# A graph layer with mixture-of-experts attention: the last tiles of z transposed in halves between gates and the first queries and keys

## The chip, the cores and the metric

The kernel runs on one core of a Trainium2 chip, in one launch. The metric is the device time of the execution in microseconds (us), the median of several runs. A core has five engines with instruction streams of their own: TensorE (PE in the profile; its weight loads are PEld), VectorE (DVE), ScalarE (ACT), GpSimd (POOL) and SyncE (SP), which here issues most of the DMAs. An engine executes its stream in order, so an instruction that waits holds up everything behind it on its engine.

## The reference

1250 nodes with 1024 values each go through a graph layer and then through an attention layer whose values and outputs are mixtures of experts:

```python
edge_index = stack([src, dst])                      # 40000 edges, and one self loop per node
x  = x + gnn(layernorm(x), edge_index, W, b)        # h = x W^T + b; sum over edges, weighted by degrees^-1/2
z  = layernorm(x)                                   # x is called x1 in the kernel
q  = rope(einsum('bsd,hdp->bhsp', z, Wq))           # 16 heads of 64
k  = rope(einsum('bsd,hdp->bhsp', z, Wk))
gv = gate(z, Wsel_v); go = gate(z, Wsel_o)          # sigmoid scores of 8 experts, all but the best two set to 0
v  = einsum('bsd,bhse,hedp->bhsp', z, gv, Wv)
o  = softmax(q k^T / 8) v
y  = z + einsum('bhsp,bhse,hepd->bsd', o, go, Wo)
y  = layernorm(y, ln1_g, ln1_b)
y  = layernorm(y + relu(y W1 + b1) W2 + b2, ln2_g, ln2_b)
out = x + y
```

## The kernel before

All large products are made in three matmuls: each operand is split into a rounded part (`hi`, type fp32r) and what is left (`lo`), and `dot` (L152 to L156) adds hi x hi, hi x lo and lo x hi in a PSUM tile. A split costs a copy on ACT (the rounding) and a subtraction on DVE (the rest): for a weight block of 128x1024, loaded by SP into a raw buffer of `w_raw` (two of them), they are L138 and L144; for a transposed tile they are L190 and L191.

**Stages in order of time.** The edges are counted into a matrix `at16`, beside h = W x + b (to 232 us). `sums(ts)` (L478) makes the graph sums of tile t of 125 nodes: 40 matmuls of 512 columns, then on DVE the scaling and the residual (`x1`, in a buffer named `y`), and the layer norm (`normalize`: two `bn_stats` and their aggregate, a square root on ACT, the reciprocal, the last step), which gives z. Both x1 and z are stored to DRAM (`x1_d`, `z_d`; each `move` is two DMAs, of 112 and of 13 rows). The last sum's matmul ends on PE at 314.05 us.

What follows needs z with its 1024 values on the partitions: `turn_z` (L520) calls `transposed` (L181), which takes a tile in two halves, each of four PE transposes (L187) into one bank of `side` (PSUM, three banks in turn), one ACT copy into `hi` and one DVE subtraction into `lo` (a tile that straddles columns 512 has two of each). The result is `zT`, in two pieces: zT00/zT01 for the first `CUT` = 512 nodes and zT10/zT11 for the other 738. The first four of ten tiles are turned during the sums (L527 to L531). The other six come after them: `rest_of_z` (L542) loads each from `z_d` into a `w_raw` buffer and turns it.

- `queries_keys` (L599) has 48 pieces: 16 blocks of weights (`wqk`, 8 pairs of heads, two halves of their dimensions), and for each three column chunks of 512, 384 and 354 nodes. A piece is 8 x 3 matmuls into one of four `mm` banks, then the rotation by cos and sin for every other block (L643 to L648, four DVE operations), the split and the regrouping (L649 to L658); after a third chunk the results go to DRAM (`kq_d`).
- `gates` (L551) has ten pieces: 8 x 3 matmuls of 256 columns for 128 nodes (`dot` L580, in a `side` bank), the sigmoid on ACT (L583), then 14 DVE operations that find the two best of eight (`pick`, L558, twice, and L585 to L590), the product for the values' gates (`gate_v`), and one for the outputs' gates, which `turn_gates` (L568) transposes one gate later into `po` and ACT copies into `gT`. Its weights `wsel` are two blocks, split at its start (L556).

**Order.** L678 to L683 set the order in which these are issued: first tile 4 of z, then the other five between the first two pieces of queries and keys, then a gate after every third piece. But in this stage the order written is no more than a priority: a scheduler with a cost model places the instructions of every engine. From the attention on (`attention`, `values`, `outputs`) the order of every engine is written by hand (`tc.manual_schedule`, L1106); the last part (`outputs`' rest from L1131 and `feed_forward`, L1031: layer norm, two products with 512 hidden values, layer norm and residual) is left to the scheduler again. There L1018 adds each finished output product to `acc` on DVE.

**Buffers.** Weight parts come from `ring`, a list of pools used in turn: two slots of `ring0` and, after the sums, three of `ring1` (L533). `hpool` holds h in two parts and two z tiles.

Of the kernel before, what the change touches and what calls it, by code (L numbers as in the profile page):

```python
# [72 lines left out]
def gnn_ffn_kernel(  # L73
# [106 lines left out]

    def transposed(targets, y, psum_tile):  # L181

        for half in range(2):
            p = psum_tile([P, 4, KT])
            for k in range(4):
                d0 = (4 * half + k) * P
                nc.tensor.transpose(p[:, k, :], y[:, d0 : d0 + P], ident[:KT, :KT])  # L187
            for hi, lo, c0, cols in targets:
                to = (slice(None), slice(4 * half, 4 * half + 4), slice(c0, c0 + cols.stop - cols.start))
                nc.scalar.copy(hi[to], p[:, :, cols])  # L190
                nc.vector.tensor_tensor(lo[to], p[:, :, cols], hi[to].bitcast(F32), ALU.subtract)  # L191

    def broadcast_row(pool, row, name):

        b = pool.tile([P, D], F32, name=name)
        nc.sync.dma_start(b, bass.AP(tensor=row.tensor, offset=row.offset, ap=[[0, P], [1, D]]))
        return b


    with ExitStack() as gctx:  # L200
# [277 lines left out]
        def sums(ts):  # L478
# [19 lines left out]
            for t, pp in zip(ts, pps):  # L498
                x1 = stream.tile([P, D], F32, name="y")
                move(x1, xres_d[t])  # L500
                for half in range(2):
                    cols = slice(512 * half, 512 * half + 512)
                    nc.vector.scalar_tensor_tensor(x1[:KT, cols], pp[half], ds[:KT, t : t + 1], x1[:KT, cols],
                                                   op0=ALU.mult, op1=ALU.add)
                z = hpool.tile([P, D], F32, name="z", bufs=2)
                normalize(z[:KT], x1[:KT], "g")
                move(z_d[t], z)
                move(x1_d[t], x1)
                zs.append(z)
# [9 lines left out]

        def turn_z(t, z):  # L520

            c0, c1 = KT * t, KT * (t + 1)
            mid = min(max(CUT, c0), c1)
            targets = [(*zT[k], a - CUT * k, slice(a - c0, b - c0)) for k, a, b in ((0, c0, mid), (1, mid, c1)) if b > a]
            transposed(targets, z, side_bank)

        for t in range(2, NT):  # L527
            new = sums([t])
            if t - 2 < NZ:
                turn_z(t - 2, zs.pop(0)[:KT])  # L530
                zs += new  # L531

    ring += [ctx.enter_context(tc.tile_pool(name="ring1", bufs=3))] * 3  # L533
    zpool2 = z2_ctx.enter_context(tc.tile_pool(name="zpool2", bufs=1, side="right"))
# [6 lines left out]

    def rest_of_z():  # L542

        for t in range(NZ, NT):
            z = raws[0].tile([P, D], F32, name="w_raw")[:KT]
            move(z, z_d[t])
            turn_z(t, z)
            yield


    def gates(wpool, tmp):  # L551
        first_wins = wpool.tile([P, NX], F32, name="first_wins")
        nc.gpsimd.iota(first_wins, pattern=[[-1, NX]], base=NX, channel_multiplier=0,
                       allow_small_or_imprecise_dtypes=True)
        gT = wpool.tile([P, N], F32, name="gT")
        sel = [weights(wsel[k]) for k in range(2)]  # L556

# [15 lines left out]

        before = None
        for t in range(NT):
            n = min(P, N - P * t)
            p = side_bank([n, 2 * P])
            for d in range(ND):
                w = [part[:, 2 * P * (d % 4) : 2 * P * (d % 4 + 1)] for part in sel[d // 4]]
                dot(p, z_of(t, d), w, d == 0, d == ND - 1)  # L580
            s, a, b, c = (tmp.tile([P, 2 * H, NX], F32, name=k)[:n] for k in ("s", "a", "b", "chosen"))
            m = tmp.tile([P, 2 * H], F32, name="m")[:n]
# [7 lines left out]
            nc.vector.tensor_tensor(a[:, H:, :], s[:, H:, :], c[:, H:, :], ALU.mult)  # L590
            if before is not None:
                turn_gates(t - 1, before)
            before = a
            yield
        turn_gates(NT - 1, before)
        nc.sync.dma_start(g_d, gT)


    def queries_keys(tab, work):  # L599
        cos_s = tab.tile([P, N], F32, name="cos_s")  # L600
        nc.sync.dma_start(cos_s, cos)
        sin_s = tab.tile([P, N], F32, name="sin_s")
        nc.sync.dma_start(sin_s, sin)
        turn16 = [(i + NROT // 2) % NROT for i in range(NROT)]
# [19 lines left out]
        pieces = [(i, k) for i in range(H) for k in range(3)]  # L624
        pieces[:6] = [(0, 0), (1, 0), (0, 1), (0, 2), (1, 1), (1, 2)]
        tiles = {}
        for i, k in pieces:
# [7 lines left out]
            for d in range(ND):  # L635
                dot(p, [part[:, P * d : P * (d + 1)] for part in w],
                    [part[:, d, c0 : c0 + n] for part in zT[part2]], d == 0, d == ND - 1)
            at_ = slice(CUT * part2 + c0, CUT * part2 + c0 + n)
            if other:
# [38 lines left out]
    with tc.tile_pool(name="qktab", bufs=1) as tab, tc.tile_pool(name="qkwork", bufs=2) as work, \  # L678
            tc.tile_pool(name="gatet", bufs=2) as tmp:
        turns, rest = queries_keys(tab, work), rest_of_z()  # L680
        next(rest)
        interleave(islice(turns, 2), rest, 1, 2 / 5)
        interleave(turns, gates(tab, tmp), 1, 3)  # L683

# [524 lines left out]
```

## Time and profile before

| | |
|---|---|
| median of 3 runs | 2961.8 us (2959.9 to 2963.07) |
| profiled execution, its own time | 2961.16 us |
| its span, first to last instruction | 2959.4 us |
| mean granted TensorE clock | 0.986 |
| PE busy | 2849.7 us (96%), 14018 instructions |
| DVE busy | 2120.9 us (72%), 3588 |
| ACT busy | 993.0 us (34%), 1706 |
| POOL busy | 569.1 us (19%), 945 |
| DMA | 385.45 MB, mean 130 GB/s |

By stages: sums to 314.05 us, the last tiles of z and first queries and keys to 364, queries, keys and gates to 591.6, values, attention and outputs to about 2780, the last part to 2959.

How the lines are read: a page's engine rows give 40 equal slices of the span (74 us each), each digit the busy share in tenths. A row of the time line is start, duration, engine, line of the code, operation, output tile <- inputs, shape, and in brackets the idle time of the engine before it and whose result ended it. A row of waits is the waiting engine, tile and line, the instruction it waited for, and the sum, number and longest of the waits. `PEclk` is the granted TensorE clock, 1.00 being full speed. Matmuls overlap in the pipeline, so a matmul's duration is longer than its distance from the one before; that distance is what counts when PE is full.

### The profile page before, as it was taken

The page shows a single profiled execution, that of the slowest core. Times are in us where ns is not written, and L with a number is a line of the kernel's source. Part 1 is how long each engine was busy: PE and PEld are TensorE (multiplying, and loading weights), DVE is VectorE, ACT ScalarE, POOL GpSimd, SP SyncE. Part 2 cuts the span into 40 slices and gives each one's busy share as a digit, 9 for nine tenths or more (in the row PEclk, how much of TensorE's full clock was granted, in tenths as well). Part 3 has the DMA queues.
Part 4 walks back from the last instruction along what each step waited for, and adds up shares of the span by engine and source line. Part 5 has one row for each costly group of instructions (what it writes and reads, how often), then busy time and mean ns, then how long its engine had stood idle before and what let it go on. Part 6 is the DMA issues. An engine that isn't in the chain of part 4 may idle for free. (4 is left out here: it accounts for less than half of the span.)

```text
span 2959.4 us, 40398 instructions
## 1 busy us (share of the span) xinstructions
PE 2849.7 (96%) x14018; PEld 2349.2 (79%) x14018; DVE 2120.9 (72%) x3588; ACT 993.0 (34%) x1706; POOL 569.1 (19%) x945
## 2 busy tenths in 40 slices
PE   6989899999999999999999999899999999999998
PEld 4767699978887887788888888777777777777787
DVE  7974487647777777778778787866666666656885
ACT  5772233324343433434434344321111111111222
POOL 2000011113333333333333333310000000000113
PEclk9999899999999999999999999999999999999999
DMA  3114456644555554555555555884444444444312
GB/s 117 56 44 146 150 163 169 197 99 125 151 132 134 134 142 124 144 140 147 130 152 139 144 132 129 209 217 128 114 119 121 114 123 117 115 121 119 112 52 88
DMA packets 229320, 385.45 MB, mean 130 GB/s; under 512 B 43369, under 2 KB 176489, under 8 KB 228946
## 3 DMA queue, kind: packets, MB, share of 16 engines
q1 hardware_dynamic: 176898, 273.49, 33.3%
q0 software_dynamic: 51888, 104.18, 14.6%
q10 hardware_dynamic: 320, 5.12, 0.6%
q8 instruction: 111, 1.82, 0.3%
q14 instruction: 103, 0.84, 0.1%
HBM read 220.73 MB, written 62.16 MB: 96 GB/s over the span
## 5 line engine op out<-in xcount | busy, mean ns | idle before, releaser
L154 PE MATMUL mm<-w_hi,go_hi 128*125 128x512 f32 x1280 | 507.9, 397 | 4.5 <-DVE zT L1018 3.4
L155 PE MATMUL mm<-w_lo,zT 128*128 128x512 f32 (+1 forms) x1280 | 506.4, 396 | 4.3 <-DVE w_lo L144 3.9
L155 PE MATMUL mm<-w_lo,go_hi 128*125 128x512 f32 x1280 | 508.8, 398 | 0.0
L154 PE MATMUL mm<-w_hi,zT 128*128 128x512 f32 (+1 forms) x1280 | 506.5, 396 | 1.0 <-ACT w_hi L138 1.0
L156 PE MATMUL mm<-w_hi,go_lo 128*125 128x512 f32 x1280 | 506.7, 397 | 0.7 <-DVE go_lo L960 0.7
L156 PE MATMUL mm<-w_hi,zT 128*128 128x512 f32 (+1 forms) x1280 | 505.3, 395 | 0.0
L755 ACT CAST att_hi<-turned 128x512 fp32r<-128x512 f32 x400 | 239.5, 621 | 455.5 <-DVE turned L798 279.5
L736 POOL DMA_DIRECT2D turned<-p x640 | 342.5, 542 | 80.8 <-ACT p L725 44.3
L1018 DVE TENSOR_TENSOR zT<-zT,mm 125x512 f32<-125x512 f32 x256 | 175.5, 686 | 220.5 <-PE mm L156 216.3
L798 DVE STREAM_TRANSPOSE turned<-turned 128x1280 f32<-128x1280 f32 x160 | 232.4, 1490 | 135.7 <-DMA q<-kq_d 57.5
L958 ACT CAST go_hi<-gb 128x500 fp32r<-128x500 f32 x160 | 98.3, 615 | 660.1 <-PE mm L155 289.1
L724 DVE TENSOR_REDUCE most<-side 128x1 f32<-128x1250 f32 x160 | 231.0, 1444 | 108.2 <-PE side L721 106.7
L725 ACT ACTIVATE p<-side,most 128x1250 f32<-128x1250 f32 x160 | 209.2, 1307 | 289.4 <-DVE most L724 284.7
L154 PEld LDWEIGHTS mm<-w_hi,go_hi 128*125 128x125 f32 x1280 | 239.1, 187 | 66.0 <-DVE zT L1018 4.1
L156 PEld LDWEIGHTS mm<-w_hi,go_lo 128*125 128x125 f32 x1280 | 238.9, 187 | 61.9 <-DVE go_lo L960 1.2
L155 PEld LDWEIGHTS mm<-w_lo,go_hi 128*125 128x125 f32 x1280 | 238.7, 186 | 59.2
L156 PEld LDWEIGHTS mm<-w_hi,zT 128*128 128x128 f32 (+1 forms) x1280 | 238.0, 186 | 59.5
L155 PEld LDWEIGHTS mm<-w_lo,zT 128*128 128x128 f32 (+1 forms) x1280 | 238.4, 186 | 44.3 <-DVE w_lo L144 9.4
L154 PEld LDWEIGHTS mm<-w_hi,zT 128*128 128x128 f32 (+1 forms) x1280 | 238.3, 186 | 35.8 <-ACT w_hi L138 1.2
L760 DVE TENSOR_TENSOR att_lo<-turned,att_hi 128x512 fp32r<-128x512 f32 x400 | 262.4, 682 | 0.0
L778 PE MATMUL po<-att_hi,v 128*128 128x256 f32 (+1 forms) x800 | 215.0, 290 | 33.8 <-ACT o L785 33.5
L144 DVE TENSOR_TENSOR w_lo<-w_raw,w_hi 128x1024 fp32r<-128x1024 f32 x154 | 189.5, 1231 | 43.6 <-ACT w_hi L138 43.3
(234 smaller groups left out, 4611.3 us busy)
## 6 DMA issues: line engine op xcount, KB each, us to landing
turned<-p SPq DMA_DIRECT2D x640, 80.0 KB
turned<-p POOLq DMA_DIRECT2D x640, 80.0 KB, 3.3
gb<-g_d SPq DMA_DIRECT2D x160, 250.0 KB
w_raw<-in_wv SPq DMA_DIRECT2D x64, 512.0 KB
w_raw<-in_wo SPq DMA_DIRECT2D x64, 512.0 KB
q<-kq_d POOLq DMA_DIRECT2D x80, 256.0 KB, 4.3
oc<-o_d SPq DMA_DIRECT2D x160, 125.0 KB
kq_d<-qk_hi SPq DMA_DIRECT2D x64, 156.2 KB
```

What stands on the lines that cost most here:

```text
L144: (lo_engine or nc.vector).tensor_tensor(lo, raw, hi.bitcast(F32), ALU.subtract)
L154: nc.tensor.matmul(p, lhsT=lhs[0], rhs=rhs[0], start=start, stop=False)
L155: nc.tensor.matmul(p, lhsT=lhs[0], rhs=rhs[1], start=False, stop=False)
L156: nc.tensor.matmul(p, lhsT=lhs[1], rhs=rhs[0], start=False, stop=stop)
L724: nc.vector.tensor_reduce(most, side[:, :N], AX.X, ALU.max, negate=True)
L725: nc.scalar.activation(p[:, (2 * n + i) % 3, :N], side[:, :N], AF.Exp, bias=most, accum_out=inverse[h][:, 2 * c + i : 2 * c + i + 1])
L736: queue.dma_start(t[NB * a : NB * (a + 1), :, KA * b : KA * (b + 1)], both[NB * b : NB * (b + 1), :, KA * a : KA * (a + 1)])
L755: nc.scalar.copy(hi, x)
L760: nc.vector.tensor_tensor(lo, x, hi.bitcast(F32), ALU.subtract)
L778: nc.tensor.matmul(po, lhsT=v_of[h][:rows, t, :], rhs=part[:rows, :, NB * b : NB * (b + 1)], start=(first and b == 0 and part is parts[0]) ...
L798: nc.vector.transpose(turned[n][:, i], turned[n][:, i])
L1018: nc.vector.tensor_tensor(acc[t][:, cols], acc[t][:, cols], p, ALU.add)
```

## The change

- `transposed` and `turn_z` take the halves that they are to do. `rest_of_z(pool)` goes on by half tiles, and loads each z tile two tiles ahead of its use, into two buffers `z` of the pool `tmp` (that of the gates' small tiles) instead of the `w_raw` buffers.
- The gates' weights `wsel` are loaded and split during the sums, when tile 5 of them is issued, into the two slots of `ring0`; for queries and keys the ring has only the three slots of `ring1`, and `ring0` is put back after. For room, z tiles 6 to 9 of the sums are made in `w_raw` buffers. `first_wins` (the order in which equal scores win) is made at the kernel's start.
- A gate takes an `mm` bank instead of a `side` bank, and is transposed three gates later, with four `a` buffers.
- A piece of queries and keys can be left after half of its matmuls; the first six pieces stand in another order. The tables cos and sin are loaded after the first gate.
- In the stretch after the sums PE's order is written by hand (`manual_schedule` for PE alone; the other engines stay with the scheduler): gates, half tiles and half pieces in turn, by the tuple `order`. After it, a gate comes after every sixth half piece.

As built, PE's order after the last sum is: gate 0, half tile 4a, gate 1, 4b, gate 2, 5a, half a piece, 5b, half, 6a, gate 3, 6b, half, 7a, half, 7b, 8a, half, 8b, half, 9a, half, 9b, half, and so on. Every half tile waits for the DVE subtraction of the half before it. z tile 4's load waits for the last graph sum on PE, tile 6's for tile 4's second half. SP issues in the order: z tile 4, tile 5, x1's last store, a `wqk` block, z's last store, cos, sin, z tile 6, two `wqk` blocks, tile 7, two more blocks, tiles 8 and 9. On ACT, gate 0's sigmoid stands ahead of the last normalisation's square root. The instructions of attention, values and outputs stand in the same order as before up to the last 40 output matmuls, ahead of which 23 of the feed-forward's first matmuls now come.

```diff
@@ -178,9 +178,9 @@
         nc.vector.scalar_tensor_tensor(out, x, mean, scale, op0=ALU.subtract, op1=ALU.mult)
         nc.vector.scalar_tensor_tensor(out, out, rs, shift, op0=ALU.mult, op1=ALU.add)
 
-    def transposed(targets, y, psum_tile):
-
-        for half in range(2):
+    def transposed(targets, y, psum_tile, halves=(0, 1)):
+
+        for half in halves:
             p = psum_tile([P, 4, KT])
             for k in range(4):
                 d0 = (4 * half + k) * P
@@ -195,6 +195,9 @@
         b = pool.tile([P, D], F32, name=name)
         nc.sync.dma_start(b, bass.AP(tensor=row.tensor, offset=row.offset, ap=[[0, P], [1, D]]))
         return b
+
+    first_wins = base.tile([P, NX], F32, name="first_wins")
+    nc.gpsimd.iota(first_wins, pattern=[[-1, NX]], base=NX, channel_multiplier=0, allow_small_or_imprecise_dtypes=True)
 
     with ExitStack() as gctx:
@@ -502,7 +505,7 @@
                     cols = slice(512 * half, 512 * half + 512)
                     nc.vector.scalar_tensor_tensor(x1[:KT, cols], pp[half], ds[:KT, t : t + 1], x1[:KT, cols],
                                                    op0=ALU.mult, op1=ALU.add)
-                z = hpool.tile([P, D], F32, name="z", bufs=2)
+                z = hpool.tile([P, D], F32, name="z", bufs=2) if t < 6 else raws[0].tile([P, D], F32, name="w_raw")
                 normalize(z[:KT], x1[:KT], "g")
                 move(z_d[t], z)
                 move(x1_d[t], x1)
@@ -517,20 +520,24 @@
         zpool = z_ctx.enter_context(tc.tile_pool(name="zpool", bufs=1, side="right"))
         zT = [[zpool.tile([P, ND, CUT], F32R, name=f"zT0{k}") for k in range(2)]]
 
-        def turn_z(t, z):
+        def turn_z(t, z, halves=(0, 1)):
 
             c0, c1 = KT * t, KT * (t + 1)
             mid = min(max(CUT, c0), c1)
             targets = [(*zT[k], a - CUT * k, slice(a - c0, b - c0)) for k, a, b in ((0, c0, mid), (1, mid, c1)) if b > a]
-            transposed(targets, z, side_bank)
+            transposed(targets, z, side_bank, halves)
 
         for t in range(2, NT):
             new = sums([t])
+            if t == 5:
+                sel = [weights(wsel[k]) for k in range(2)]
             if t - 2 < NZ:
                 turn_z(t - 2, zs.pop(0)[:KT])
                 zs += new
 
-    ring += [ctx.enter_context(tc.tile_pool(name="ring1", bufs=3))] * 3
+
+    first_two = ring[:]
+    ring[:] = [ctx.enter_context(tc.tile_pool(name="ring1", bufs=3))] * 3
     zpool2 = z2_ctx.enter_context(tc.tile_pool(name="zpool2", bufs=1, side="right"))
     zT.append([zpool2.tile([P, ND, N - CUT], F32R, name=f"zT1{k}") for k in range(2)])
 
@@ -539,21 +546,23 @@
         k = t if t < NZ else t - NZ
         return [part[:, d, P * k : min(P * (k + 1), part.shape[2])] for part in zT[t >= NZ]]
 
-    def rest_of_z():
-
-        for t in range(NZ, NT):
-            z = raws[0].tile([P, D], F32, name="w_raw")[:KT]
-            move(z, z_d[t])
-            turn_z(t, z)
-            yield
+    def rest_of_z(pool):
+
+        zs = []
+        for t in range(NZ - 2, NT):
+            if t >= NZ:
+                turn_z(t, zs[0], (0,))
+                yield
+                turn_z(t, zs.pop(0), (1,))
+            if t + 2 < NT:
+                zs.append(pool.tile([P, D], F32, name="z")[:KT])
+                move(zs[-1], z_d[t + 2])
+            if t >= NZ:
+                yield
 
     def gates(wpool, tmp):
-        first_wins = wpool.tile([P, NX], F32, name="first_wins")
-        nc.gpsimd.iota(first_wins, pattern=[[-1, NX]], base=NX, channel_multiplier=0,
-                       allow_small_or_imprecise_dtypes=True)
         gT = wpool.tile([P, N], F32, name="gT")
-        sel = [weights(wsel[k]) for k in range(2)]
 
         def pick(chosen, v, m):
 
@@ -571,14 +580,15 @@
             nc.tensor.transpose(pg, a[:, H:, :].rearrange("p h e -> p (h e)"), ident[:n, :n])
             nc.scalar.copy(gT[:, P * t : P * t + n], pg)
 
-        before = None
+        before = []
         for t in range(NT):
             n = min(P, N - P * t)
-            p = side_bank([n, 2 * P])
+            p = bank([n, 2 * P])
             for d in range(ND):
                 w = [part[:, 2 * P * (d % 4) : 2 * P * (d % 4 + 1)] for part in sel[d // 4]]
                 dot(p, z_of(t, d), w, d == 0, d == ND - 1)
-            s, a, b, c = (tmp.tile([P, 2 * H, NX], F32, name=k)[:n] for k in ("s", "a", "b", "chosen"))
+            s, a, b, c = (tmp.tile([P, 2 * H, NX], F32, name=k, bufs=4 if k == "a" else 2)[:n]
+                          for k in ("s", "a", "b", "chosen"))
             m = tmp.tile([P, 2 * H], F32, name="m")[:n]
             nc.scalar.activation(s.rearrange("p h e -> p (h e)"), p, AF.Sigmoid)
             pick(c, s, m)
@@ -588,19 +598,16 @@
             nc.vector.tensor_tensor(gate_v[:n, t, :].rearrange("p (h e) -> p h e", h=H), s[:, :H, :], c[:, :H, :],
                                     ALU.mult)
             nc.vector.tensor_tensor(a[:, H:, :], s[:, H:, :], c[:, H:, :], ALU.mult)
-            if before is not None:
-                turn_gates(t - 1, before)
-            before = a
+            before.append(a)
+            if t > 2:
+                turn_gates(t - 3, before.pop(0))
             yield
-        turn_gates(NT - 1, before)
+        for t in range(NT - 3, NT):
+            turn_gates(t, before.pop(0))
         nc.sync.dma_start(g_d, gT)
 
-    def queries_keys(tab, work):
-        cos_s = tab.tile([P, N], F32, name="cos_s")
-        nc.sync.dma_start(cos_s, cos)
-        sin_s = tab.tile([P, N], F32, name="sin_s")
-        nc.sync.dma_start(sin_s, sin)
+    def queries_keys(cos_s, sin_s, work):
         turn16 = [(i + NROT // 2) % NROT for i in range(NROT)]
 
         chunks = [(0, 0, CUT), (1, 0, 3 * P), (1, 3 * P, N - CUT - 3 * P)]
@@ -622,7 +629,7 @@
 
         pieces = [(i, k) for i in range(H) for k in range(3)]
-        pieces[:6] = [(0, 0), (1, 0), (0, 1), (0, 2), (1, 1), (1, 2)]
+        pieces[:6] = [(0, 0), (1, 0), (0, 1), (1, 1), (0, 2), (1, 2)]
         tiles = {}
         for i, k in pieces:
             j, other = divmod(i, 2)
@@ -635,6 +642,8 @@
             for d in range(ND):
                 dot(p, [part[:, P * d : P * (d + 1)] for part in w],
                     [part[:, d, c0 : c0 + n] for part in zT[part2]], d == 0, d == ND - 1)
+                if d == ND // 2 - 1:
+                    yield
             at_ = slice(CUT * part2 + c0, CUT * part2 + c0 + n)
             if other:
                 raw, scale = p, HD**-0.5
@@ -677,10 +686,19 @@
 
     with tc.tile_pool(name="qktab", bufs=1) as tab, tc.tile_pool(name="qkwork", bufs=2) as work, \
             tc.tile_pool(name="gatet", bufs=2) as tmp:
-        turns, rest = queries_keys(tab, work), rest_of_z()
-        next(rest)
-        interleave(islice(turns, 2), rest, 1, 2 / 5)
-        interleave(turns, gates(tab, tmp), 1, 3)
+        cos_s, sin_s = (tab.tile([P, N], F32, name=name) for name in ("cos_s", "sin_s"))
+        turns, rest, gate = queries_keys(cos_s, sin_s, work), rest_of_z(tmp), gates(tab, tmp)
+
+        order = (gate, rest, gate, rest, gate, rest, turns, rest, turns, rest, gate, rest, turns, rest, turns, rest,
+                 rest, turns, rest, turns, rest, turns, rest, turns)
+        with tc.manual_schedule(engines={mybir.EngineType.PE}):
+            next(gate)
+            nc.sync.dma_start(cos_s, cos)
+            nc.sync.dma_start(sin_s, sin)
+            for what in order[1:]:
+                next(what)
+        interleave(turns, gate, 1, 6)
+    ring[:0] = first_two
```

## The prediction

> **What bounds the kernel now.** I read the page first, for which engine is full and where not, then the table by stretches around the change, then who TensorE waited for there, then the time line of that stretch.
>
> ```profile
> PE 2849.7 (96%) x14018; PEld 2349.2 (79%) x14018; DVE 2120.9 (72%) x3588; ACT 993.0 (34%) x1706; POOL 569.1 (19%) x945
> ...
> PE   6989899999999999999999999899999999999998
> ```
>
> TensorE (PE) sets the time: 96% busy, and its slices are full except at the start and in the fifth slice (296 to 370 us, an 8). Two stretches of the table by stretches, the columns being named in its header:
>
> ```profile
> core 0: us, PE busy (x) PEld busy (x) DVE busy (x) ACT busy (x) POOL busy (x), PEclk, DMA share, GB/s
> 314.05:364.00 49.95, 35.99 (x152) 29.48 (x151) 22.34 (x39) 13.87 (x24) 0.14 (x1) 0.79 0.36 120
> 364.00:591.60 227.60, 226.93 (x1301) 212.14 (x1300) 174.27 (x388) 75.38 (x158) 29.29 (x60) 1.00 0.61 176
> ```
>
> 314.05 is where the last graph sum ends on PE, 591.6 where the first value product begins. In the first stretch, which I call the head, PE is idle for 14.0 of 49.95 us and its granted clock is 0.79; VectorE (DVE) is 45% busy, and the DMA engines move 120 GB/s. After it PE is full. PE's waits in the head:
>
> ```profile
> PE side L187 <- DVE zT L191: 10.2, 5, 4.1
> PE mm L154 <- ACT zT L190: 2.7, 4, 1.5
> ```
>
> They are the transposes of z's last six tiles (L187 into `side`). The time line of PE shows the form:
>
> ```profile
> 338.20 0.65 PE L187 MATMUL side<-ident,w_raw 125*128 125x125 f32 x4 [1.55 <-DVE zT L191]
> 340.23 1.10 PE L187 MATMUL side<-ident,w_raw 125*128 125x125 f32 x4 [1.38 <-DVE zT L191]
> 342.71 1.09 PE L187 MATMUL side<-ident,w_raw 125*128 125x125 f32 x4 [1.38 <-DVE zT L191]
> ```
>
> Each half tile (four transposes) waits until the half before it was copied by ScalarE (ACT) and subtracted by DVE, though `side` has three banks; the halves follow at 2.0 to 2.5 us, and the same transposes take 1.1 instead of 0.59 us: the clock has dropped.
>
> What the head loses: warm, a 512-column matmul follows the last at 0.2285 us (376.21 to 381.70 for 24), 384 at 0.1755, 354 at 0.1625, a gate's 256 at 0.1135, and a half tile takes 0.35. From 314.05 to 591.6 that is 16 x 24 x (0.2285 + 0.1755 + 0.1625) = 217.5 for queries and keys, 10 x 24 x 0.1135 = 27.2 for gates, 12 x 0.35 = 4.2 for half tiles, about 1 for the gates' own transposes: 250 of 277.5. So 27.5 us are lost, 25.1 of them by the same subtraction before 364: 13.9 waiting, the rest at the half clock (twelve 512-column matmuls at 0.427 from 323.1 to 329.35, some twenty of 384 at 0.32) and in the pipeline's restarts.
>
> **The change, part by part.**
>
> *Removed.* The head's order by the scheduler: half tiles in a row, z reloaded into the weight buffers, gates only from 367 on. With it go up to 25.1 us.
>
> *Put in its place, on PE* (order by hand; work the same): gate, half, gate, half, gate, half, half a piece of queries, and so on, so that 2.1 to 2.7 us of matmuls stand between two half tiles. A wait stays: in the built order each half tile still waits for DVE's subtraction of the one before. PE is in order, so everything behind a half tile waits with it.
>
> *Moved to DVE.* Four gates come into the head. What must have passed DVE before the eleventh half tile: four gates at 12 x 0.42 + 2 x 0.29 = 5.6 (rows of L562 to L590), 22.5; ten subtractions, mostly at 0.67, 7.1; three weight splits at 1.22, 3.7; the first query and key pieces, 4.2 + 1.4; the last normalisation, 1.0: 39.9 us in some 86 operations. Independent neighbours overlap by 0.08 (331.38, 331.97 for one of 0.68), so about 33. I start it at 320.0, because the last tile's statistics still come first (y, 1.41, from 314.0), and the first gate's scores come late: the gate ends on PE at 316.8, then ACT does a table load (1.28), the sigmoid (0.39), a second table load back for the square root (1.28) and the root (0.29), and only then the first copy of z. So DVE frees the eleventh half tile at 353.0. PE's own work up to there: gates 10.9, half tiles 3.5, four half pieces of 2.74, two of 2.1, three small transposes 0.3: 29.9. It loses 353.0 - 314.05 - 29.9 = **9.1 us**, of which about 1.1 is the wait for the reloaded tile below. DVE, idle for 27 us of the old head, is the new bound; from 353 on PE is full again as it was from 364. Gain: 25.1 - 9.1 = **16.0 us**.
>
> I cost the two added table loads by the row (1.28, and the next instruction began when its input was there). The Trainium skill, "ScalarE: Activation LUTs", What ACT_TABLE_LOAD costs, adds a drain of some 1.38 us to each. By it the two switches would take 2.8 us more out of the chain, and the sum would be 13.2; no run here shows the drain, as ACT waited for PE behind the one load.
>
> *DMAs.* z tiles 4 and 5, loaded at 285 and 295 before, now go into a pool over memory that the graph sums free, and wait for their last matmul. A 512 KB load alone lands in 3.5 to 3.9 us (issued 362.79, used 366.68), so tile 4 is there at 318.0, 1.1 after the first gate; upper end 2 us. Behind it on SP's queue stand tile 5, x1's store, the first weights, z's last store, both tables, and six more loads: 8 MB in some 40 us, 200 GB/s, against 278 measured from 285 to 300 (share 0.90). It fits, with little room: ACT's casts of three weight blocks stand ahead of z copies, so a late block delays z. Ends: 0, and +7 us if each of the three is late by 2 to 2.5.
>
> *Gate weights* load earlier, while the sums keep PE full. Their casts stand on ACT ahead of the sums' third `at` cast, which had to wait until 234.8 anyway. DVE frees the old buffers at 226.9; two loads and two casts later it is about 233.5. Nothing, +1 if the loads take a us longer.
>
> *Later gates* take `mm` banks instead of `side` and come every third piece as before: 0, ends -1 and +1, for PE lost only 2.4 from 364 to 591.6. The weight ring has three slots for queries and keys, five with the gates' two before: nothing, since each block serves 13.6 us of PE. `first_wins` made at the start: nothing, POOL is idle.
>
> *Behind.* Attention and outputs keep their order, and PE is full there, so the gain is handed through. The scheduler's last part does change: 23 of the feed-forward's first matmuls (2.6 us) move ahead of the last 40 output matmuls. There PE waits now:
>
> ```profile
> 2818.93 0.79 PE L154 MATMUL mm<-w_hi,go_hi 128*125 128x512 f32 x1 [3.42 <-DVE zT L1018]
> ```
>
> That is 3.4 us of waiting for DVE's evictions (DVE is 100% busy from 2800 to 2820) and, behind it, twelve 512-column matmuls at 0.427 instead of 0.2285 (2818.9 to 2823.8), 2.4 us. The matmuls that move there, 23 x 0.1135 = 2.6 us, fill most of the gap; but DVE's work, which is late, stays as much, and its order changes too. I take **2.0 us** gained; ends 5 gained and 4 lost.
>
> *Sum.* The profiled execution took 2961.2 (its span 2959.4 and 1.8 around it), 0.6 below the median 2961.8. 2961.2 - 16.0 - 2.0 = 2943.2; the median's 0.6 put back, **2944**. With the head's loss between 4 and 16 us (9.1; five less if DVE starts two earlier, at 318, and overlaps three more; seven more for late blocks) and the last part's ends, that is from 2936 (5 and 3 less) to 2957 (7 and 6 more).
>
> **The rivals.**
>
> *Loads late (0.20).* Three weight blocks, the reloaded tiles and two tables share SP's queue. For it: 8 MB in 40 us, casts ahead of z copies on ACT, and at 200 GB/s a 512 KB block takes 2.6 us, as long as a half piece. Against: 278 GB/s was reached. The head then loses 16: **2951**.
>
> *The saving is lost again (0.08).* What the head gains must come through 2,300 us of PE work. For it: attention starts at 654 with a 3.1 us wait, and the tail's order is new. Against: PE is full between, so only an order that costs DVE 14 us or more behind the head would do it, **2956 to 2961**. That the change does not do what it says belongs here: nothing, if halves wait as before; but the gates between them need only z's first 512 rows, long there.
>
> *Slower: the clock (0.07).* The granted clock in the head is 0.79, and it falls at gaps: a matmul-free stretch from 318.98 to 323.11 was followed by matmuls at 0.427 until 329.35, one from 352.06 to 356.7 by half speed until 359.7, and 12 half tiles in a row brought it down until 349.6. It came back after 6.2, 5.1 and 3.0 us of matmuls. In the changed order PE works in bursts of 2.1 to 2.7 us between gaps of 0.7 to 2.6, so if one gap drops the clock, no burst may be long enough to bring it back before 353. The 29.9 us of work then take up to 0.427 / 0.2285 = 1.87 times as long, + 26; DVE's chain hides 9 of it at most, and PE's waits between bursts stay in part: a loss of 25 + 13 = 38 against 25.1, **2972**. It decides for slower from the point at which more than 60% of the head's matmuls (18 of 29.9 us, + 16) run at half clock. Against: gaps of 0.76 and 1.3 us (314.2 to 316.2) did not drop it; the longest stretch without a product in the changed order, two halves in a row after the seventh tile, is 2.6 + 0.7 = 3.3 us, just under the shortest that dropped it (3.42, in the last part).
>
> The Trainium skill, "TensorE: Matmul & The Clock Gate", Part 1: The HAM clock gate, says that an idle window of about 3.4 us throttles, that a busy one as long must be sustained for release, and that transposes do not count as busy. The rows above agree. By it alone the 3.3 us stand just at the edge, and a drop there, at some 345, would cost one window at half clock, about 1.7 us (an estimate from that page); the sum would be 14.3 instead of 16.0.
>
> **How the numbers follow.** 0.65 for the forecast (2936 to 2948), 0.20 for late loads (2948 to 2955), 0.08 for a saving lost again, 0.07 for the clock. A difference of 0.2% is 5.9 us, about what a measurement of this kernel can tell from no change. Faster by more holds the first two and a little of the third: 0.86; within it, 0.07; slower, 0.07. The range 2936 to 2956, the upper end's last us left out, holds the first two cases, 0.85, less a little for ends I have not seen: 0.8.
>
> **What would show it.** In the changed profile, from the last graph sum on: PE waits for some 9 us, not 14, in gaps of 0.7 to 2.6 ahead of half tiles, ended by zT's subtraction on DVE; the granted clock stays near 1.0; DVE is over 90% busy, from 45%; each half tile's transposes take 0.35 to 0.6 us; the first value product begins at 575 to 577 instead of 591.6. z's tile 4 lands some 4 us after the last sum. In the tail the 3.42 us wait is under 1. I am wrong if the clock falls below 0.9 in the head; if PE there waits for `w_hi`, or ACT for a DMA; if DVE has idle time while PE waits, which would mean that ACT's table loads or copies are the chain and not DVE's sum; or if the first value product is 14 us earlier and the end is not.

## The result and the profile after

The changed kernel takes 2948.13 us (median of 6 runs, 2942.87 to 2952.0) against 2963.78 us for the kernel before (6 runs, 2959.9 to 2969.11): 15.65 us less, a ratio of 0.9945 with a 95% interval from 0.993 to 0.9959. The forecast was 2944 us, 17.8 us less. The profiled execution took 2949.87 us, its span is 2948.1.

The page of the kernel after, its engines and the slices of TensorE:

```profile
PE 2845.5 (97%) x14018; PEld 2346.9 (80%) x14018; DVE 2118.5 (72%) x3588; ACT 996.7 (34%) x1708; POOL 570.3 (19%) x945
...
PE   6989999999999999999999999899999999999998
```

The work of TensorE and VectorE is the same (14018 and 3588 instructions again); ScalarE has two more, the added table loads. The fifth slice is no longer an 8 (in the second profile of this kernel, `again` below, it still is). The table by stretches, the first row for the 50 us after the last graph sum and the second from there to the last query and key product (the columns are those of the table shown before):

```profile
312.28:362.28 50.00, 43.15 (x273) 39.38 (x272) 41.37 (x98) 20.94 (x37) 0.00 (x0) 0.97 0.51 161
362.28:575.72 213.44, 213.44 (x1181) 197.98 (x1180) 152.04 (x328) 69.68 (x146) 29.41 (x60) 1.00 0.62 181
```
In the first row TensorE is idle for 6.9 us where it was 14.0, its clock is 0.97 where it was 0.79, and VectorE is busy for 41.4 us of 50. In the second there is no idle time. TensorE's waits from 312.28 to 364, all of them:

```profile
PE side L187 <- DVE zT L191: 4.7, 4, 2.2
PE side L187 <- DMA z<-z_d: 1.5, 1, 1.5
PE po L580 <- ACT gT L581: 0.6, 1, 0.6
```

Half tiles on TensorE's time line (start, duration, then the idle time before and what ended it; the one at 329.00 did not wait):

```profile
316.66 0.62 PE L187 MATMUL side<-ident,z 125*128 125x125 f32 x4 [1.53 <-DMA z<-z_d]
320.79 0.65 PE L187 MATMUL side<-ident,z 125*128 125x125 f32 x4 [0.68 <-DVE zT L191]
325.70 0.65 PE L187 MATMUL side<-ident,z 125*128 125x125 f32 x4 [1.42 <-DVE zT L191]
329.00 0.59 PE L187 MATMUL side<-ident,z 125*128 125x125 f32 x4
...
346.41 0.65 PE L187 MATMUL side<-ident,z 125*128 125x125 f32 x4 [2.23 <-DVE zT L191]
```

Where the profiled executions differ, along TensorE's time line (us; "stretch" is from the start of the first graph sum to the end of the last query and key product; the sums in it took 99.4 to 100.4 us from profile to profile, most of the difference in their first tile, so the time from their end stands below it; "last part" is from the first transposes of acc to the end; "again" is the changed kernel once more):

| | before | after | again |
|---|---|---|---|
| to the first graph sum | 213.9 | 212.0 | 213.4 |
| stretch | 378.0 | 363.7 | 365.3 |
| of that, from the end of the last graph sum | 277.7 | 263.4 | 265.8 |
| values, attention, outputs, up to the last part | 2191.1 | 2196.5 | 2190.7 |
| in this, TensorE's waits for attention (`po` for `o`) | 33.8 | 38.1 | 30.2 |
| last part | 176.4 | 175.9 | 176.1 |

So the change gave 14.3 and 12.7 us in the stretch (14.2 and 11.9 counted from the last sum), 0.3 to 0.5 in the last part, and nothing that can be told from chance elsewhere. The attention's waits move by several us from profile to profile (25 to 38 us over all the kernels below); this is why the experiments are measured by their stretch, which is read from the profile, and the totals stand beside it. Each kernel has one profile, the changed one two, which differ by 1.5 us in the stretch and by 2.4 from the last sum; so smaller differences between two kernels can't be told from chance.

### The profile page after: what moved, and what is told of

The parts are those of the page before. It is cut to its first block, busy times and chain, and to the rows that moved or that the text cites. A ratio compares the mean times of both kernels' runs of the same rounds, so it can differ in the third digit from the quotient of the medians.

```text
span 2948.1 us, 40387 instructions
## 1 busy us (share of the span) xinstructions
PE 2845.5 (97%) x14018; PEld 2346.9 (80%) x14018; DVE 2118.5 (72%) x3588; ACT 996.7 (34%) x1708; POOL 570.3 (19%) x945
## 5 line engine op out<-in xcount | busy, mean ns | idle before, releaser
L155 PE MATMUL mm<-w_lo,zT 128*128 128x512 f32 (+2 forms) x1360 | 528.9, 389 | 3.8 <-DVE w_lo L144 3.3
L154 PE MATMUL mm<-w_hi,zT 128*128 128x512 f32 (+2 forms) x1360 | 529.7, 390 | 0.8 <-ACT w_hi L138 0.8
L156 PE MATMUL mm<-w_hi,zT 128*128 128x512 f32 (+2 forms) x1360 | 528.4, 389 | 0.0
L156 PEld LDWEIGHTS mm<-w_hi,zT 128*128 128x128 f32 (+1 forms) x1360 | 253.1, 186 | 59.9
L155 PEld LDWEIGHTS mm<-w_lo,zT 128*128 128x128 f32 (+1 forms) x1360 | 253.3, 186 | 43.9 <-DVE w_lo L144 8.6
L154 PEld LDWEIGHTS mm<-w_hi,zT 128*128 128x128 f32 (+1 forms) x1360 | 253.7, 187 | 35.6 <-ACT w_hi L138 1.0
L796 PE MATMUL po<-att_hi,v 128*128 128x256 f32 (+1 forms) x800 | 216.1, 291 | 38.1 <-ACT o L803 38.0
```

Of the source, the lines that this page charges most:

```text
L154: nc.tensor.matmul(p, lhsT=lhs[0], rhs=rhs[0], start=start, stop=False)
L155: nc.tensor.matmul(p, lhsT=lhs[0], rhs=rhs[1], start=False, stop=False)
L156: nc.tensor.matmul(p, lhsT=lhs[1], rhs=rhs[0], start=False, stop=stop)
L796: nc.tensor.matmul(po, lhsT=v_of[h][:rows, t, :], rhs=part[:rows, :, NB * b : NB * (b + 1)], start=(first and b == 0 and part is parts[0]) ...
```

## The experiments

All kernels compute the whole result. "Ratio" is against the kernel before on the same chip, with its 95% interval, from all the runs; it need not be the ratio of the two medians. TensorE's own work in the stretch is some 352 us, an estimate: 100.3 for the sums as measured before the change, and about 252 for gates, half tiles, queries and keys from the distances between their matmuls. The expectations of the first four runs count from the last sum, the others from the first; both are in the table.

| kernel | stretch | from the last sum | median, us | before, us | ratio |
|---|---|---|---|---|---|
| before | 378.0 | 277.7 | | | |
| changed | 363.7 | 263.4 | 2948.13 | 2963.78 | 0.9945 (0.993 to 0.9959) |
| again | 365.3 | 265.8 | 2947.24 | 2965.76 | 0.9931 (0.9907 to 0.9954) |
| sched | 375.2 | 275.7 | 2959.22 | 2965.76 | 0.9976 (0.9965 to 0.9987) |
| blocks | 384.5 | 284.2 | 2969.78 | 2965.76 | 1.0006 (0.9994 to 1.0018) |
| onetable | 364.0 | 264.6 | 2941.81 | 2965.76 | 0.993 (0.9905 to 0.9955) |
| held | 359.1 | 259.8 | 2938.86 | 2967.14 | 0.9921 (0.9892 to 0.9951) |
| indep | 356.0 | 256.6 | 2943.01 | 2967.14 | 0.9922 (0.9902 to 0.9942) |
| heldd | 359.0 | 259.6 | 2940.32 | 2967.14 | 0.9907 (0.9891 to 0.9924) |
| heldall | 356.1 | 255.8 | 2934.59 | 2967.14 | 0.9892 (0.9876 to 0.9909) |
| beforeindep | 363.3 | 263.3 | 2952.08 | 2968.01 | 0.9952 (0.9935 to 0.9969) |
| schedindep | 358.2 | 258.8 | 2945.05 | 2968.01 | 0.9929 (0.9913 to 0.9946) |
| best | 354.4 | 255.0 | 2928.56 | 2968.01 | 0.9868 (0.9851 to 0.9884) |

**again.** No edit.

> The changed kernel once more, for a second profile and more times. Measure for all runs: the stretch from the end of the last graph sum on TensorE to the end of the last query and key product (before 277.7 us, after 263.4), as the total moves by several us from run to run through the attention's waits. Theory (the gain of some 14 us comes from this stretch alone, the attention's waits of 33 to 38 us and the last part are chance or unchanged): 263.4 within 1 us, the last part from the first transposes of acc to the end 175.5 to 176.5 as in both profiles, time 2945 to 2951. Rival (the attention or the last part was changed by the new order): the attention's waits at 37 to 39 again, or a last part shorter by 2.

265.8 from the last sum, last part 176.1, attention's waits 30.2, time 2947.24: the last part and the time are as the theory said, the stretch is 1.4 above its bound, and neither sign of the rival came. Of the 2.4 us between the two profiles the waits are 0.8 (6.9 and 7.7). The rest is the clock: in the first profile it fell once, for 3.4 us (347.8 to 351.2), in the second twice (from 339.7 and from 349.9), and 3.4 us at half speed lose some 1.7 (an estimate, half of it).

**sched.** The order by hand taken away:

```diff
-        with tc.manual_schedule(engines={mybir.EngineType.PE}):
-            next(gate)
...
+        next(gate)
+        nc.sync.dma_start(cos_s, cos)
+        nc.sync.dma_start(sin_s, sin)
+        for what in order[1:]:
+            next(what)
```

> The same pieces, loads and buffers, but TensorE's order in the stretch is left to the scheduler as before (no order by hand). Theory (the interleave on TensorE is what pays): the scheduler again sets half tiles in rows, TensorE waits 4 to 10 us more, the stretch is 268 to 275 us. Rival (early gates and z tiles loaded ahead pay, the hand's order does not matter): 262 to 265.

275.7 from the last sum, 0.7 above the theory's upper end and far from the rival. Early gates and reloads ahead bring 2.0 us against the kernel before, no more than two profiles of one kernel differ by; the order by hand brings another 9.9 to 12.3 (against the two profiles of the changed kernel). Half tiles on the time line of sched:

```profile
340.83 1.09 PE L187 MATMUL side<-ident,z 125*128 125x125 f32 x4 [4.82 <-DVE zT L191]
343.71 1.10 PE L187 MATMUL side<-ident,z 125*128 125x125 f32 x4 [1.79 <-DVE zT L191]
346.63 1.09 PE L187 MATMUL side<-ident,z 125*128 125x125 f32 x4 [1.82 <-DVE zT L191]
```

**blocks.** The same by hand, with half tiles in rows:

```diff
-        order = (gate, rest, gate, rest, gate, rest, turns, rest, turns, rest, gate, rest, turns, rest, turns, rest,
-                 rest, turns, rest, turns, rest, turns, rest, turns)
+        order = (gate,) * 3 + (rest,) * 6 + (gate,) + (turns,) * 4 + (rest,) * 2 + (rest,) * 4 + (turns,) * 4
```

> The order by hand, but in blocks: three gates, six half tiles in a row, a gate, four half pieces, six half tiles in a row, then the pieces. Same instructions, same work on every engine. Theory (what stands between two half tiles hides the copy and the subtraction of the one before, and keeps the clock): the twelve half tiles follow at 2.0 to 2.5 us, some 8 to 11 us more waiting and the clock at half speed for 7 to 14 us: 272 to 280. Rival (VectorE's total work bounds the stretch, whatever the order): 263 to 266.

The stretch is 384.5, worse than before; from the last sum it is 284.2, 4.2 above the theory's range, so the theory had the direction and not the size. On blocks' time line the first halves waited longest:

```profile
326.88 1.09 PE L187 MATMUL side<-ident,z 125*128 125x125 f32 x4 [5.57 <-DVE zT L191]
334.06 1.10 PE L187 MATMUL side<-ident,z 125*128 125x125 f32 x4 [6.08 <-DVE zT L191]
336.53 1.09 PE L187 MATMUL side<-ident,z 125*128 125x125 f32 x4 [1.38 <-DVE zT L191]
```

So VectorE's total, which is the same here, is not what bounds the stretch by itself: its subtraction stands in a queue behind the gates' choices, and TensorE had nothing beside it to do.

**onetable.** `tc.issue_after` puts the first sigmoid behind the last square root on ScalarE, so that two table loads go.

> The first gate's sigmoid is issued behind the last normalisation's square root on ScalarE, so that ScalarE loads one table instead of three (two loads of 1.28 us less at the start of the stretch). Theory (the stretch is bound by VectorE's work from the first gate on, and VectorE starts with the first sigmoid, which does not come earlier): 0.5 to 1.5 us less, 262 to 263. Rival (ScalarE's loads are the chain, as the waits at the second and third half tile, 0.68 and 1.42, say): 2 to 3 us less, 260.4 to 261.4.

264.6 from the last sum, against 263.4 and 265.8: neither. The half tile 4b no longer waits, but 5a waits 2.08 and 6b 1.33; the waits moved on. (The total is lower for the attention's waits, 30.1.)

**held.** The same operations on VectorE, the choices of the first four gates behind the last subtraction:

```diff
...
+            late.append((t, s))
+            if t > 3:
+                while late:
...
+                    with tc.issue_after(last_lo[0].ins) if t == 4 else nullcontext():
+                        choose(*late.pop(0))
```

> Same work, but VectorE's choices for the first four gates (22.5 us of operations) are held behind the subtraction of the last half tile; their scores wait in five buffers. Measure: from the first graph sum on TensorE to the end of the last query and key product (before 378.0 us, the changed kernel 363.7 and 365.3 in two profiles, TensorE's own work some 352). Theory (VectorE's work is the bound of the stretch): its wait for half tiles nearly vanishes, 355 to 358, the clock stays at 1.0, total 5 to 8 us less than the changed kernel. Rival (each half tile waits for the chain of copy and subtraction of the one before, whatever else VectorE does): 362 to 365. Second rival (the choices come back as waits later among queries and keys): less waiting in the head, but over 0.5 us of waits after it, and 361 to 364 in all.

359.1, between theory and rival. Rows of 50 us that begin 0.9 us after the last sum's end, of held and then of indep:

```profile
310.54:360.54 50.00, 44.99 (x295) 41.38 (x294) 29.62 (x60) 21.28 (x35) 0.00 (x0) 1.00 0.52 161
```

```profile
310.62:360.62 50.00, 47.86 (x313) 44.38 (x312) 45.05 (x108) 22.41 (x39) 0.00 (x0) 1.00 0.53 163
```

In held VectorE is busy for 29.6 us of 50, and TensorE still waits 2.7 us for its subtractions:

```profile
PE side L189 <- DVE zT L193: 2.7, 3, 1.6
PE side L189 <- DMA z<-z_d: 2.3, 2, 1.9
```

An engine with 20 us to spare can't be the bound by its work; what is left of the wait is the chain of one half tile. The choices were a part of the wait all the same: it was 4.7 and 5.6 us with them.

**indep.** Three tiles in place of three slices of one:

```diff
-        side = psums[0].tile([P, 3 * 512], F32, name="side")
-        turns_of_side = cycle(range(3))
+        s_ctx = p_ctx.enter_context(ExitStack())
+        halves_p = s_ctx.enter_context(tc.tile_pool(name="halves", bufs=3, space=PSUM))
...
-            c0 = 512 * next(turns_of_side)
-            found = side[: shape[0], c0 : c0 + int(np.prod(shape[1:]))]
-            return found if len(shape) == 2 else found.rearrange("p (a b) -> p a b", b=shape[2])
+            return halves_p.tile(shape, F32, name="half")
...
+    s_ctx.close()
+    side = p_ctx.enter_context(tc.tile_pool(name="sides", bufs=1, space=PSUM)).tile([P, 3 * 512], F32, name="side")
```

> The half tiles get three PSUM banks of their own, tracked one by one, so that a half tile waits only for the bank three halves before and not for the subtraction of the half just before. Nothing else is changed. Same measure. Theory (VectorE's work is the bound): the four waits in front of half tiles (4.7 us) go, but the query pieces that need the columns, or banks, wait instead: 361.5 to 364.5. Rival (the dependency through the one side tile is the bound): 357 to 360.

356.0: the rival, 1.0 below its range. VectorE does more in the 50 us than in any other kernel (45.05, its row above), and TensorE waits for it no more; what it waits for is the reload:

```profile
PE half L187 <- DMA z<-z_d: 2.0, 2, 1.6
```

The plainest sign is when a half tile starts against the end of the subtraction of the half before, both read from the time lines. In the kernel before none of the eleven starts earlier, and six start 0.05 to 0.06 us after it; in the changed kernel none is earlier and four start 0.05 to 0.06 after. In indep eight start earlier, by up to 2.48 us. Here half tile 4b on TensorE, and the last subtraction of 4a on VectorE, which had not even begun:

```profile
317.48 0.59 PE L187 MATMUL half<-ident,z 125*128 125x125 f32 x4
317.58 0.62 DVE L191 TENSOR_TENSOR zT<-half,zT 128x452 fp32r<-128x452 f32 x1
```

The scheduler also set VectorE's operations in another order there, which this edit can't hold still. But that order does not bring the subtractions sooner: from the start of a half tile's transposes to the end of its subtraction it takes 3.5 us on average over the twelve, against 2.9 in both profiles of the changed kernel.

**heldd.** As held, and z's tile 4 is transposed from where the sums leave it:

```diff
+                if t == 4:
+                    z = gate_flat[:, :D]
...
+        zs = [gate_flat[:KT, :D]]
...
```

> As held, and z's tile 4 is not loaded again: the graph sums' last step writes it into the memory of gate_v, free until the first choice is made, and it is transposed from there. Same measure. Theory: the wait of 1.5 us for the load at the first half tile goes and nothing comes in its place, 1.0 to 1.6 less than held. Rival (ScalarE, which then still does the first sigmoid and the square root with three table loads, is late for the first halves instead): within 0.5 of held.

359.0: the rival. The 1.9 us wait for the load went, and the second half tile waited 1.73 us for the first one's copy and subtraction (two of ScalarE's three table loads stand before them).

**heldall.** heldd with indep's and onetable's edits.

> As heldd, with the half tiles' own banks of indep and the first sigmoid behind the last square root (one table load instead of three). Same measure. Theory: what is left of waits in the head are the chains of the first halves; both changes together bring 0.5 to 2.5 less than heldd, down to 353 to 355, next to TensorE's own work. Rival (what is left is the loads of weights or tables): within 0.5 of heldd, with waits on w_lo or on turned.

356.1, 2.9 less than heldd, but above the theory's 353 to 355, and not to be told from indep alone (255.8 and 256.6 from the last sum). What it waits for now, on TensorE's time line, is the first block of weights:

```profile
323.39 0.50 PE L155 MATMUL mm<-zT,w_hi 128*128 128x512 f32 x1 [0.93 <-ACT w_hi L139]
324.65 0.50 PE L157 MATMUL mm<-zT,w_lo 128*128 128x512 f32 x1 [0.53 <-DVE w_lo L145]
```

**beforeindep.** indep's edit in the kernel before, and nothing of the change.

> The kernel before, with nothing but the three banks of its side tile made tiles of their own, tracked one by one, while z's tiles and the gates use them; everything else as it was, the order by the scheduler. Measure: from the first graph sum on TensorE to the end of the last query and key product (before 378.0 us, changed 363.7 and 365.3, changed with own banks 356.0). New theory (a half tile's wait for the subtraction of the half just before it, which only the tracking of the side tile as one asks for, is most of what the head lost, and the change hid a part of it): 360 to 368 without any of the change. Rival (the interleave with gates and half pieces is needed all the same, since halves in a row are bound by VectorE's 0.67 us each and reloads come late): 370 to 377.

363.3, as the new theory said, and what the whole change gives; ratio 0.9952 against its 0.9945 and 0.9931. TensorE now makes up to three half tiles in one go. The long wait is that of the seventh, which needs the bank of the fourth and starts 0.11 us after the fourth's subtraction ends (behind this wait the clock was at half speed for 10.2 us):

```profile
313.29 1.44 PE L187 MATMUL half<-ident,w_raw 125*128 125x125 f32 x12
326.32 1.44 PE L187 MATMUL half<-ident,w_raw 125*128 125x125 f32 x12
332.94 1.90 PE L187 MATMUL half<-ident,w_raw 125*128 125x125 f32 x8 [5.17 <-DVE zT L191]
```

**schedindep.** The changed kernel with the own banks and without the order by hand.

> The changed kernel with the own banks, but TensorE's order in the head left to the scheduler. Same measure. New theory (with own banks the order by hand is worth little): 356 to 360. Rival (the order by hand keeps its 11 us against the scheduler's): 364 to 368.

358.2, in the new theory's range: with own banks the order by hand is worth 2.2 us (against indep), which is within the spread, where it was worth 9.9 to 12.3 without them.

**best.** heldall, and the fourth gate ahead of the first half piece:

```diff
+        order = (gate, rest) * 4 + (turns, rest) * 4 + (rest, turns, rest, turns, rest, turns, rest, turns)
```

> The own banks, the first four gates' choices held behind the last half tile, z's tile 4 not reloaded, one table load, and the fourth gate moved ahead of the first half piece, so that the first weight block, for which TensorE waited 1.5 us with half speed behind it, has 2.8 us more. Same measure; TensorE's own work is some 352 to 353. New theory (only chains of the first halves and the first block were left): 353 to 354.5. Rival (the next block or tile is late instead): 355.5 to 356.5. Total against before: 24 to 32 us less.

354.4, within the theory's range, though only 0.8 us below heldall when counted from the last sum; the only wait left in the 50 us is 1.01 us for a reloaded tile. The kernel takes 2928.56 us, 39.5 less than before on the same chip and more than the 24 to 32 expected; ratio 0.9868 (0.9851 to 0.9884). 23.6 us of this are the stretch (22.7 from the last sum); the profiled execution took 2933.9 us, 27.3 less than that of before, and what the rest of the median's difference is made of stays open.

## Why the prediction came out right, and where it did not

*What bounds the kernel, and what goes.* Right: the whole gain lies between the last graph sum and 364, and PE hands it through. Of the 25.1 us lost there, 14.2 and 11.9 came back, against 16.0 forecast. The total was forecast lower by 17.8 and fell by 15.65, but it moves by more than the 2 us between them from run to run, so that it came so near is partly luck.

*The new loss in the head, 9.1 us.* From the last sum to the last half tile it was some 11 us (46.1 us, less gates 13.1, half tiles 4.2, pieces 17.5, small transposes 0.4). Waits: 1.53 for the reloaded tile (1.1 forecast), 4.7 behind subtractions in four gaps of 0.41 to 2.23 (0.7 to 2.6 forecast), 0.6 for a gate's transpose that ScalarE had not copied. The other 4 us are the clock (some 1.7) and restarts, which the sum had put at nothing. The eleventh half tile came 41.1 us after the last sum, 39.0 were forecast.

*"DVE, idle for 27 us of the old head, is the new bound."* **This step failed, though its size was nearly right.** It added up 33 us of VectorE's work and took the end of that sum for the time at which TensorE is set free. VectorE did become full: over the first row's 50 us it is 83% busy, where over 90% was forecast, but from 318.51 (the last normalisation's reciprocal) to the end of the tenth subtraction at 352.54 it is busy for 33.4 of 34.0 us. Yet the eleventh half tile, at 353.23, did not wait for it. In indep VectorE does all of this work, at 90% busy, and TensorE does not wait for it; in held it does over a quarter less (29.6 us for 41.4), and TensorE still waits 2.7 us. What bounds both kernels is the wait named one part earlier ("each half tile still waits for DVE's subtraction of the one before", "though `side` has three banks") and then not priced: three banks are one tile, tracked as one. VectorE's queue decides how long that wait takes, and so both readings gave nearly the same number. That the sum of VectorE's work came so near the right time was luck in this respect. The change leaves this wait and puts work beside it; taking it away gives as much in the kernel before (363.3) and some 7 to 9 us more in the changed one (356.0).

*Two more table loads.* Priced at 1.28 each, without a drain. ScalarE's time line of the changed kernel:

```profile
315.19 1.28 ACT L593 ACT_TABLE_LOAD   x1 [9.24 <-PE mm L156]
316.49 0.39 ACT L593 ACTIVATE s<-mm 128x256 f32<-128x256 f32 x1
316.89 1.28 ACT L166 ACT_TABLE_LOAD   x1
318.19 0.30 ACT L166 ACTIVATE sdg<-mvg,eps 125x1 f32<-125x1 f32 x1
```

The second load begins 0.01 us after the sigmoid's end, and the root 0.02 after the load. The drain of some 1.38 us that the Trainium skill adds ("ScalarE: Activation LUTs", What ACT_TABLE_LOAD costs) is not there, so the sum of 13.2 had no ground, though the measured gain is near it. And the two loads were not on the path that set the head's length: onetable takes them away and the stretch is not shorter (364.0).

*The clock.* The rival that it stays down did not come; a part of it did. It fell for 3.4 us once (after the wait of 2.23 between two half tiles, at 347.8) and for 3.4 us twice in the second profile, where that window and 0.8 us more of waits make 2.4 us; the bursts of some 2.5 us between gaps were enough to bring it back. By the rule of the Trainium skill ("TensorE: Matmul & The Clock Gate", Part 1: The HAM clock gate) the prediction had put one window of that length at this place; both traces agree (347.8 and 349.9), and the second has one more, which it had not seen. That transposes do not count as busy stands in Part 4 of that page, not in Part 1, and no run here tests it by itself. One reading of the old head was wrong: not twelve half tiles stood in a row before its clock came back at 349.6, but four from 336.05 on and a fifth behind a single product.

*Loads late.* ScalarE waited 0.54 and 0.67 us for weight blocks, and no half tile is seen to be late for it. The rival's 7 us did not come.

*The last part, 2.0 us.* Wrong: 0.3 to 0.5. TensorE's waits there sum to 7.6 us, where they were 6.4. The 23 matmuls moved ahead do not fill the gap, since the first of them waits for the same thing:

```profile
2808.97 0.58 PE L154 MATMUL mm<-sT,w_hi 128*128 128x256 f32 x1 [3.55 <-DVE zT L1036]
```

It too needs an `mm` bank, and VectorE, which frees these, is late. The prediction had seen that VectorE's work is late there, and yet took moved matmuls for cover. (Over all the kernels the last part took 173.6 to 178.7 us, so a gain of a few tenths can't be told from none.)

*Gate weights early, later gates, ring.* Right: the sums take 100.30 us before and after (99.44 in again), and from 362.28 on PE does not wait.

## What to carry to other kernels

When an instruction waits for the last user of a buffer, ask first whether it needs that buffer: slices of one tile may be tracked as one, and separate tiles then take the wait away where a new order only covers it. A sum of an engine's work says when it could be done, not who waits for it; test it by holding back work that nobody waits for, and by loosening the wait with all the work left in. Before matmuls are moved into a gap, look at what ended the gap: if they need the same thing, they wait as well.

## What had not been expected

- An edit of a few lines in the kernel before (beforeindep) is worth as much as the whole change: 14.7 us of the stretch, 14.4 from the last sum.
- Between two profiles of the same kernel TensorE's waits for the attention differ by 8 us (38.1 and 30.2) and the half-speed windows by one, so a single total can't weigh an edit of 0.2%.
- A wait of 0.57 us and one of 1.28 us, with two small transposes between, were followed by a half-speed window in the second profile (339.7); alone, a wait of 1.42 us was not. What decides between the two is open.
